# Marks of used channels made on chip, and the down marks scattered with the gate pieces, in a gated attention and feed-forward block

## The chip, the core and the metric

The kernel runs on one core of a Trainium2 chip. Its engines are TensorE (PE, with its weight loads shown as PEld), VectorE (DVE), ScalarE (ACT), GpSimd (POOL) and SyncE (SP, which here only issues DMAs). The metric is the device time of one execution in microseconds (us). For the kernel before, the median of three runs is 751.65 us (749.36 to 752.27).

## What is computed

The reference takes x (8 batches, 256 rows, 512 channels), applies a layer norm and cross-attention with 16 heads to a context of 256 rows, adds the result through a tanh gate, and then a feed-forward part with 1408 inner channels. The feed-forward part quantises to fp8, and it reorders channels by two index lists before it does so:

```python
def _qlinear(qx, scale_x, scale, W, idx, out_idx=None):
    Wr = W[:, idx]
    w_scale = jnp.max(jnp.abs(Wr), axis=1, keepdims=True) / FP8_MAX
    qw = _fp8(Wr / w_scale)
    y = qx * scale_x @ (qw * w_scale).T * scale
    if out_idx is not None:
        y = y[:, out_idx]
    return y
...
qx, sx, sc = _reorder_quantize_x(xf, up_reorder_index)
g = _qlinear(qx, sx, sc, w_gate, up_reorder_index, out_idx=down_reorder_index)
u = _qlinear(qx, sx, sc, w_up, up_reorder_index, out_idx=down_reorder_index)
t = jax.nn.silu(g) * u
qt, st, sct = _reorder_quantize_x(t, down_reorder_index)
y = _qlinear(qt, st, sct, w_down, down_reorder_index)
```

The row maxima are taken over the channels that an index list names. A list may in principle name a channel twice and another never. The kernel therefore needs marks: for each of the 512 input channels whether `up_reorder_index` names it, and for each of the 1408 inner channels whether `down_reorder_index` does. A weight row is multiplied by the marks before its maximum is taken.

## The kernel before

All work is in tiles of 128 partitions. A batch of x is two such tiles of 512 channels. The program has a first part (loads, the four attention weights, keys, values and queries of batch 0), a middle part, and the feed-forward part at the end. The middle part loops over 8 batches with 8 pairs of heads each. For a pair it forms scores on PE (L528), subtracts the row maximum on DVE (`sn`, L543), takes the exponential on ACT (`pr`, L553), transposes (L569) and multiplies by the values (L587). Between the pairs stand slots that hold the projections of the next batch, and "pieces" of the feed-forward weights: 11 rows of tiles of the gate weight (`prep_up`, L344), then a gather of the whole by the up index (`gather_up`, L360), the same for the up weight, then four pieces of the down weight (`prep_down`, L370) and its gather. The source order is only a wish: a scheduler moves instructions between the engines' queues as their dependences allow, and each engine then runs its own queue in order. A DMA is queued on the engine that issues it: SP, ACT or POOL.

What the change and the steps of the prediction touch:

- The small loads on ACT's queue: the biases bq_c, bk_c, bv_b, bo_b (L110 to L116), the two gates (L118, L119), then the index lists `d_i` (L121) and `u_i` (L123), one word per element. ACT takes the tanh of the gates (`tg`, L724), DVE copies it (L725) and scales bo_b with it.
- `dd_i` (L137): eleven gathers on POOL that look the down index up in itself; POOL issues them as soon as d_i has landed. The gate pieces load their rows by dd_i (L346).
- `mark_held` (L321): it fills a small table in DRAM with zeros (L323), then scatters ones into it, 128 at a time (L328), each waiting for the one before since all write the same table. It is called for `held_u` (512 words, 4 scatters) and `held_d` (1408 words, 11 scatters), after the o weight is prepared.
- `load_held` (L337): SP loads held_u, spread over all partitions, as `mu_b` (L338), and held_d as `md_f` (L340), which DVE copies to `md_b` in bf16 (L341).
- A gate or up piece: POOL gathers the rows (L346) and multiplies them by mu_b (L352), DVE takes the maximum (L186), ACT and DVE quantise. The normalised x of each batch is multiplied by mu_b too (L676). A down piece: SP loads `wd` (L372), which shares one buffer with md_f, and DVE multiplies it by md_b (L373).
- The queries: PE multiplies (L485), DVE scales into `qT` (L492), POOL adds the bias (L495). The first scores need this. POOL also adds bo_b to x (L659).

Of the kernel before, what the change touches and what calls it, by code (L numbers as in the profile page):

```python
# [29 lines left out]
F32 = mybir.dt.float32  # L30
BF16 = mybir.dt.bfloat16
FP8 = mybir.dt.float8e4
I32 = mybir.dt.int32
U32 = mybir.dt.uint32
AF = mybir.ActivationFunctionType
ALU = mybir.AluOpType
# [4 lines left out]
P = 128  # L41
# [10 lines left out]
def tile_flamingo_block(  # L52
# [22 lines left out]
    nc = tc.nc  # L75
    B, S, C = x.shape
# [4 lines left out]
    KC = C // P  # L81
    IC = I // P
# [13 lines left out]
    dram = ctx.enter_context(tc.tile_pool(name="dram", bufs=1, space=DRAM))  # L96

    def ctile(shape, name, dt=F32):
        return const.tile(shape, dt, tag=name, name=name)
# [4 lines left out]
    def load_x(b):  # L104
        nc.sync.dma_start(
            x_sb[:, b * TPB : (b + 1) * TPB, :], x[b].rearrange("(t p) c -> p t c", p=P)
        )

    bq_c = ctile([P, KC], "bq_c")
    nc.scalar.dma_start(bq_c, bq.rearrange("(k p) -> p k", p=P))  # L110
    bk_c = ctile([P, KC], "bk_c")
# [5 lines left out]
    gate = ctile([P, 2], "gate")  # L117
    nc.scalar.dma_start(gate[:, 0:1], g_xattn.partition_broadcast(P))  # L118
    nc.scalar.dma_start(gate[:, 1:2], g_ffn.partition_broadcast(P))  # L119
    d_i = ctile([P, IC], "d_i", I32)  # L120
    nc.scalar.dma_start(d_i, down_idx.rearrange("(k p) -> p k", p=P))  # L121
    u_i = ctile([P, KC], "u_i", I32)
    nc.scalar.dma_start(u_i, up_idx.rearrange("(k p) -> p k", p=P))  # L123

    ident = ctile([P, P], "ident")
    make_identity(nc, ident)
# [2 lines left out]
    zeros = ctile([P, IC], "zeros")  # L129
    nc.vector.memset(zeros, 0.0)  # L130
    ones = ctile([P, 1], "ones")
    nc.vector.memset(ones, 1.0)


    dd_i = ctile([P, IC], "dd_i", I32)
    for k in range(IC):
        nc.gpsimd.indirect_dma_start(  # L137
            out=dd_i[:, k : k + 1],
            out_offset=None,
            in_=down_idx.rearrange("(r e) -> r e", e=1),  # L140
            in_offset=bass.IndirectOffsetOnAxis(ap=d_i[:, k : k + 1].bitcast(U32), axis=0),
# [6 lines left out]
    mu_b = ctile([P, C], "mu_b")  # L148
# [5 lines left out]
        n: dram.tile([C, I], BF16, tag=f"scr_{n}", name=f"scr_{n}") for n in ("gate", "up")  # L154
    }
    scr_d = dram.tile([I, C], BF16, tag="scr_d", name="scr_d")
    held_u = dram.tile([C, 1], F32, tag="held_u", name="held_u")
    held_d = dram.tile([I, 1], F32, tag="held_d", name="held_d")
    scr_x = [dram.tile([C, S], BF16, tag=f"scr_x{b}", name=f"scr_x{b}") for b in range(B)]

    def fp8_grid(rp, src, rs, dst, n, name):

        v = rp.tile([P, n], F32, tag="r_v", name=f"v_{name}")
        nc.scalar.activation(v, src, AF.Identity, scale=rs)  # L164
        a = rp.tile([P, n], FP8, tag="r_a", name=f"a_{name}")
        nc.scalar.activation(a, v, AF.Abs, scale=0.5, saturate=False)
        q = rp.tile([P, n], FP8, tag="r_q", name=f"q_{name}")
        nc.vector.tensor_scalar(q, v, F8_MAX, -F8_MAX, ALU.min, ALU.max, saturate=False)  # L168
        nc.vector.scalar_tensor_tensor(dst, a, F8_MAX / 2, q, ALU.max, ALU.mult)  # L169

    def scale_of(pool, mx, s, name):

        nc.vector.tensor_scalar(s, mx, R448, None, ALU.mult)  # L173
        rs = pool.tile([P, s.shape[-1]], F32, tag="rs", name=f"rs_{name}")
        nc.vector.reciprocal(rs, s)  # L175
        return rs
# [8 lines left out]
    def absmax(dst, src):  # L185
        nc.vector.tensor_reduce(dst, src, AX.X, ALU.max, apply_absolute_value=True)  # L186

    with ExitStack() as actx:
# [3 lines left out]
        at = actx.enter_context(tc.tile_pool(name="at", bufs=2))  # L192
        rp = actx.enter_context(tc.tile_pool(name="rp", bufs=2))
        one = actx.enter_context(tc.tile_pool(name="one", bufs=1))
        sm = actx.enter_context(tc.tile_pool(name="sm", bufs=4))
# [3 lines left out]
        def bank(name, dt=F32):  # L199
            n = 512 if dt == F32 else 1024  # L200
            return ps_m.tile([P, n], dt, tag="m", name=name)
# [33 lines left out]
        def norm_steps(t0, t1):  # L235
            steps = [partial(norm_stats, t) for t in range(t0, t1)]
            steps += [partial(norm_rstd, t0, t1)]
            steps += [partial(norm_max, t) for t in range(t0, t1)]
            return steps + [partial(norm_scales, t0, t1)]
# [20 lines left out]
        def prep_fp32(n, rows):  # L260
            for k in range(KC):
                wr = rows[k]
                pt = bank(f"pt_{n}{k}")
                for cc in range(KC):
                    nc.tensor.transpose(
                        pt[:, cc * P : (cc + 1) * P], wr[:, cc * P : (cc + 1) * P], ident
                    )
                nc.scalar.copy(
                    wTf[n][:, :, k * P : (k + 1) * P], pt.rearrange("p (c o) -> p c o", o=P)
                )  # L270
# [6 lines left out]
        def transpose_bf16(src, dst, n, name):  # L277

            pt = bank(f"tb_{name}", BF16)
            for k in range(n):  # L280
                nc.tensor.transpose(
                    pt[:, k * P : (k + 1) * P], src[:, k * P : (k + 1) * P], ident_b
                )
            nc.any.tensor_copy(dst, pt[:, : n * P].rearrange("p (k o) -> p k o", o=P))  # L284
# [10 lines left out]
        def prep_int8(n, tiles):  # L295
            for k, wr in enumerate(tiles):
                sk = s8[n][:, k : k + 1]
                absmax(sk, wr)
                rs = int8_scale(sm, sk, sk, f"w{n}{k}")
                qw = at.tile([P, C], BF16, tag="q8", name=f"qw_{n}{k}")  # L300
                round_int8(wr, rs, qw, f"w{n}{k}")
                transpose_bf16(qw, wT8[n][:, :, k * P : (k + 1) * P], KC, f"w{n}{k}")
# [15 lines left out]
                nc.vector.tensor_copy(dst[:, k0 * P : (k0 + m) * P], pb[:, : m * P])  # L318


        def mark_held(table, idx, n_idx):  # L321

            ins = nc.gpsimd.dma_start(  # L323
                table.rearrange("(k p) e -> p (k e)", p=P), zeros[:, :n_idx]
            )
            tc.keep_in_program_order(ins)
            for k in range(n_idx):
                nc.gpsimd.indirect_dma_start(  # L328
                    out=table[:, :],
                    out_offset=bass.IndirectOffsetOnAxis(  # L330
                        ap=idx[:, k : k + 1].bitcast(U32), axis=0
                    ),
                    in_=ones,
                    in_offset=None,
                )

        def load_held():  # L337
            nc.sync.dma_start(mu_b, held_u.rearrange("c e -> (c e)").partition_broadcast(P))  # L338
            md_f = one.tile([P, I], F32, tag="wd", name="md_f")
            nc.sync.dma_start(md_f, held_d.rearrange("c e -> (c e)").partition_broadcast(P))  # L340
            nc.vector.tensor_copy(md_b, md_f)  # L341


        def prep_up(n, w, k):  # L344
            wr = ld.tile([P, C], F32, tag="wr", name=f"wr_{n}{k}", bufs=2)
            nc.gpsimd.indirect_dma_start(  # L346
                out=wr,
                out_offset=None,
                in_=w,
                in_offset=bass.IndirectOffsetOnAxis(ap=dd_i[:, k : k + 1].bitcast(U32), axis=0),  # L350
            )
            nc.gpsimd.tensor_tensor(wr, wr, mu_b, ALU.mult)  # L352
            mx = sm.tile([P, 1], F32, tag="mx", name=f"mx_{n}{k}")
            absmax(mx, wr)
            rs = scale_of(sm, mx, s_w[n][:, k : k + 1], f"{n}{k}")
            qw = at.tile([P, C], BF16, tag="q8", name=f"q_{n}{k}")
            fp8_grid(rp, wr, rs, qw, C, f"{n}{k}")
            transpose_bf16(qw, wT[n][:, :, k * P : (k + 1) * P], KC, f"{n}{k}")
# [344 lines left out]
            rows_o.append(wr)  # L703
        for b in range(1, B):
            load_x(b)
        prep_fp32("k", rows_k)
        for f in norm_steps(0, TPB):
            f()
# [8 lines left out]
        for f in steps[LC + KC :]:  # L717
            f()
        prep_int8("o", rows_o)
        mark_held(held_u, u_i, KC)  # L720
        mark_held(held_d, d_i, IC)
        load_held()
        tg = wp.tile([P, 2], F32, tag="tg", name="tg")
        nc.scalar.activation(tg, gate, AF.Tanh)  # L724
        nc.vector.tensor_copy(gate, tg)  # L725
# [5 lines left out]

        so_b = wp.tile([P, C], F32, tag="so_b", name="so_b")

        pieces = [partial(prep_up, "gate", w_gate, k) for k in range(IC)]
        pieces += [partial(gather_up, "gate")]
        pieces += [partial(prep_up, "up", w_up, k) for k in range(IC)]
        pieces += [partial(gather_up, "up")]
        pieces += [partial(prep_down, k) for k in range(KC)] + [gather_down]

        def spread(slots, steps, first, end):  # L740
# [35 lines left out]
    with ExitStack() as fctx:  # L776
# [40 lines left out]
        for b in range(B):  # L817
            xg = fx.tile([P, KC, S], BF16, tag="xg", name=f"xg_{b}")
            for k in range(KC):
                nc.gpsimd.indirect_dma_start(  # L820
                    out=xg[:, k, :],
                    out_offset=None,
                    in_=scr_x[b][:, :],
                    in_offset=bass.IndirectOffsetOnAxis(ap=u_i[:, k : k + 1].bitcast(U32), axis=0),
                )
            for nt in range(TPB):
                t = b * TPB + nt
                tt = fw.tile([P, I], F32, tag="tt", name=f"tt_{t}")
                for half in range(2):
                    ph = {}  # L830
                    for n in ("gate", "up"):
                        ph[n] = ps_g.tile([P, 2, 512], F32, tag=n, name=f"p_{n}_{t}_{half}")
                        for j in range(2):
                            c0 = half * HI + j * QI
                            for k in range(KC):
# [4 lines left out]
                                    start=(k == 0),  # L840
                                    stop=(k == KC - 1),
# [15 lines left out]
                    up = fw.tile([P, HI], F32, tag="up", name=f"up_{t}_{half}")  # L857
# [88 lines left out]
```

## Time and profile before

| | us |
|---|---|
| median of three runs | 751.65 |
| profiled execution | 753.15 |
| its span | 751.4 |
| PE busy | 525.7 |
| DVE busy | 548.2 |
| ACT busy | 415.0 |
| POOL busy | 278.9 |

The span is what the profiler saw between the first and the last instruction; the profiled execution is 1.75 us longer than it. Busy times are sums over the span, and do not say which engine another one waits for. That is read from three other views: the busy time of each engine in chosen stretches of the span, the list of who waited for whom, and the timeline, in which a bracket at the end of a line gives the idle time of that engine just before the instruction and what released it. DMA-issuing instructions appear under the queue of their engine (SPq, ACTq), and those of POOL under POOL.

### The profile page before, as it was taken

Reading aid. Unit: us, or ns where it says so; the run is one execution under the profiler, and the core shown is the slowest. Engines: PE = TensorE matmul, PEld = TensorE weight load, DVE = VectorE, ACT = ScalarE, POOL = GpSimd, SP = SyncE. Lnnn points to the kernel's source line nnn. Section 1 sums busy time; section 2 is a strip of 40 time slices with the busy share of each in tenths; the row PEclk is TensorE's granted clock in tenths of the full one; section 3 lists DMA queues with packets and bytes.
Section 4 is the critical chain, followed back from the end, with each engine's and each line's share of the span. In section 5 each row is a group of like instructions: output and inputs, shape, how many; then the busy total and the mean of one; then the engine's idle time right before and its main releaser. Section 6 shows DMA issues by size and latency. Waiting matters only on the chain. (4 is left out here: it accounts for less than half of the span.)

```text
span 751.4 us, 10398 instructions
## 1 busy us (share of the span) xinstructions
PE 525.7 (70%) x3561; PEld 341.6 (45%) x3584; DVE 548.2 (73%) x1429; ACT 415.0 (55%) x957; POOL 278.9 (37%) x241
## 2 busy tenths in 40 slices
PE   3850867878978877788876765743857767777762
PEld 2620645645646545556455534431634434444421
DVE  2951789798797798797869873755567676978970
ACT  3450876858658678578576654552235434545540
POOL 3622355235135152330121015103455566655440
PEclk9995889999999989999898888766789899989985
DMA  8823031112034011010241123000100010000000
GB/s 270 305 14 42 1 120 45 41 28 85 2 117 136 1 57 57 17 55 29 92 130 39 39 78 92 1 15 14 43 14 32 25 42 29 32 25 29 30 14 28
DMA packets 27157, 42.59 MB, mean 57 GB/s; under 512 B 6528, under 2 KB 14080, under 8 KB 27104
## 3 DMA queue, kind: packets, MB, share of 16 engines
q1 hardware_dynamic: 18656, 29.17, 11.6%
q0 software_dynamic: 4864, 12.22, 6.5%
q10 hardware_dynamic: 3584, 0.54, 0.4%
q8 instruction: 28, 0.46, 0.2%
q14 instruction: 25, 0.20, 0.1%
HBM read 31.28 MB, written 10.63 MB: 56 GB/s over the span
## 5 line engine op out<-in xcount | busy, mean ns | idle before, releaser
L553 ACT ACTIVATE pr<-sn,nm 128x256 f32<-128x256 f32 x256 | 128.3, 505 | 58.1 <-DVE nm L543 45.4
L543 DVE CUSTOM_DVE_ANT_0 sn<-s,mk 128x256 f32<-128x256 f32 x256 | 98.4, 416 | 13.8 <-PE s L528 5.5
L569 PE MATMUL t<-ident,pr 128*128 128x128 f32 x512 | 83.6, 314 | 26.6 <-DVE woT L284 23.6
L836 PEld LDWEIGHTS <-xg 128*128 128x128 bf16 x512 | 52.8, 104 | 74.7 <-issue 34.8
L569 PEld LDWEIGHTS t<-ident,pr 128*128 128x128 f32 x512 | 69.4, 164 | 31.6 <-DVE woT L284 23.8
L868 POOL TENSOR_TENSOR tt<-up,sl 128x704 f32<-128x704 f32 x32 | 62.9, 1967 | 39.6 <-DVE up L858 23.8
L836 PE MATMUL p_up<-upT,xg 128*128 128x352 bf16 x256 | 51.8, 340 | 20.8 <-DVE up L858 18.2
L424 PE MATMUL pk<-cT,wkT 128*128 128x256 f32 x256 | 64.1, 403 | 2.4 <-issue 2.4
L495 POOL TENSOR_SCALAR qT<-qT,bq_c 128x256 f32<-128x256 f32 x32 | 17.7, 557 | 128.4 <-DVE qT L492 128.2
L836 PE MATMUL p_gate<-gateT,xg 128*128 128x352 bf16 x256 | 49.2, 337 | 14.7 <-DVE gs L849 7.9
L440 PE MATMUL pv<-wvT,cT 128*128 128x512 f32 x128 | 58.6, 603 | 0.0
L424 PEld LDWEIGHTS pk<-cT,wkT 128*128 128x128 f32 x256 | 50.7, 205 | 9.7 <-issue 2.7
L578 DVE COPY pT<-t 128x512 f32<-128x512 f32 x64 | 44.0, 687 | 11.3 <-PE t L569 7.7
L186 DVE TENSOR_REDUCE mxt<-tt 128x1 f32<-128x1408 f32 x16 | 25.9, 1620 | 33.6 <-POOL tt L868 33.6
L553 ACT ACTIVATION_READ_ACCUMULATOR pr<-sn,nm 128x1 f32 x256 | 49.0, 191 | 0.0
L528 PE MATMUL s<-kT,qT 32*128 32x256 f32 x512 | 41.3, 433 | 9.3 <-DVE nm L543 7.9
L576 ACT COPY pT<-t 128x512 f32<-128x512 f32 x64 | 37.0, 578 | 18.7 <-PE t L569 14.0
L883 ACT COPY qtT<-ptq 128x1024 bf16<-128x1024 bf16 (+1 forms) x32 | 22.3, 748 | 44.0 <-PE ptq L880 42.4
L886 PE MATMUL yp<-wdT,qtT 128*128 128x512 bf16 x161 | 42.6, 413 | 5.1 <-ACT qtT L883 3.1
L164 ACT ACTIVATE v_t<-tt,rs_t 128x1408 f32<-128x1408 f32 x16 | 23.5, 1468 | 39.7 <-DVE sy L890 39.7
L587 PE MATMUL poT<-pT,v 128*32 128x256 f32 x512 | 41.4, 450 | 2.0 <-DVE pT L578 1.0
L893 POOL TENSOR_TENSOR yo<-yo,x_sb 128x512 f32<-128x512 f32 x16 | 21.6, 1347 | 53.7 <-issue 44.3
(187 smaller groups left out, 1166.7 us busy)
## 6 DMA issues: line engine op xcount, KB each, us to landing
cr<-in_ctx_dram SPq DMA_DIRECT2D x8, 512.0 KB
x_sb<-in_x_dram SPq DMA_DIRECT2D x8, 512.0 KB
out_dram<-yo SPq DMA_DIRECT2D x16, 256.0 KB
wd<-in_L_ffn_w_down_dram SPq DMA_DIRECT2D x4, 704.0 KB
mk<-in_mask_BxSxS_ff_dram SPq DMA_DIRECT2D x8, 256.0 KB
scr_x<-x2T SPq DMA_DIRECT2D x8, 256.0 KB
scr_gate<-gateT SPq DMA_DIRECT2D x1, 1408.0 KB
scr_up<-upT SPq DMA_DIRECT2D x1, 1408.0 KB
```

The source lines that it names most:

```text
L424: nc.tensor.matmul(pk[:, :L], wTf["k"][:, cc, oc * P : (oc + 1) * P], cT[:, cc, :], start=(cc == 0), stop=(cc == KC - 1),)
L440: nc.tensor.matmul(pv, cT[:, cc, lt * P : (lt + 1) * P], wTf["v"][:, cc, :], start=(cc == 0), stop=(cc == KC - 1),)
L528: return nc.tensor.matmul(pss[h][:, nt, :], qT[r0 : r0 + D, oc, nt * P : (nt + 1) * P], kT[r0 : r0 + D, oc, :], start=True, stop=True,)
L543: nc.vector.tensor_tensor_reduce(out=sn[:, nt, :], in0=pss[h][:, nt, :], in1=mk[:, nt, :], scale=-1.0, scalar=3.0e38, op0=ALU.add, op1=ALU ...
L553: nc.scalar.activation(pr[:, nt, :], sn[:, nt, :], AF.Exp, bias=nm[:, nt : nt + 1], scale=-1.0, accum_out=sums[:, nt, h : h + 1],)
L569: nc.tensor.transpose(pst[:, lc, nt * P : (nt + 1) * P], pr[:, nt, lc * P : (lc + 1) * P], ident,)
L576: nc.scalar.copy(pT, pst)
L578: nc.vector.tensor_copy(pT, pst)
L587: return nc.tensor.matmul(poT[oc][r0 : r0 + D, :], v[0][:, lc, h * D : (h + 1) * D], probsT[h][:, lc, :], start=(lc == 0), stop=(lc == LC ...
L836: nc.tensor.matmul(ph[n][:, j, :QI], xg[:, k, nt * P : (nt + 1) * P], wT[n][:, k, c0 : c0 + QI], start=(k == 0), stop=(k == KC - 1),)
L868: nc.gpsimd.tensor_tensor(tt[:, cols], up, sl, ALU.mult)
L886: nc.tensor.matmul(py, qT[:, k, :], wdT[:, k, :], start=(k == 0), stop=(k == IC - 1))
```

## The change

The up marks are no longer kept in DRAM. POOL writes the numbers 0 to 511 into every partition (iota). DVE compares them with each column of u_i, which gives ones where a channel is named; PE multiplies by ones and sums over partitions and columns, so that each partition has a count of each channel; DVE limits it to 1, and that is mu_b. This is written ahead of the k weight's preparation. The down marks stay in DRAM, but the fill is written ahead of the list of pieces, each gate piece is written with one scatter, and the load of md_f is a piece of its own after the gather of the up weight. The loads of the two index lists go to the head of ACT's queue.

```diff
+    d_i = ctile([P, IC], "d_i", I32)
+    nc.scalar.dma_start(d_i, down_idx.rearrange("(k p) -> p k", p=P))
+    u_i = ctile([P, KC], "u_i", I32)
+    nc.scalar.dma_start(u_i, up_idx.rearrange("(k p) -> p k", p=P))
     bq_c = ctile([P, KC], "bq_c")
...
-    d_i = ctile([P, IC], "d_i", I32)
-    nc.scalar.dma_start(d_i, down_idx.rearrange("(k p) -> p k", p=P))
-    u_i = ctile([P, KC], "u_i", I32)
-    nc.scalar.dma_start(u_i, up_idx.rearrange("(k p) -> p k", p=P))
...
+    one_b = ctile([P, 1], "one_b", BF16)
+    nc.vector.memset(one_b, 1.0)
...
-    held_u = dram.tile([C, 1], F32, tag="held_u", name="held_u")
...
-        def mark_held(table, idx, n_idx):
-
-            ins = nc.gpsimd.dma_start(
-                table.rearrange("(k p) e -> p (k e)", p=P), zeros[:, :n_idx]
+        def held_up():
+
+            iota = one.tile([P, C], F32, tag="xm", name="iota")
+            nc.gpsimd.iota(
+                iota, [[1, C]], base=0, channel_multiplier=0, allow_small_or_imprecise_dtypes=True
             )
-            tc.keep_in_program_order(ins)
-            for k in range(n_idx):
-                nc.gpsimd.indirect_dma_start(
-                    out=table[:, :],
...
-        def load_held():
-            nc.sync.dma_start(mu_b, held_u.rearrange("c e -> (c e)").partition_broadcast(P))
+            u_f = sm.tile([P, KC], F32, tag="u_f", name="u_f", bufs=1)
+            nc.vector.tensor_copy(u_f, u_i)
+            pc = bank("count_u")
+            for k in range(KC):
+                oh = at.tile([P, C], BF16, tag="q8", name=f"oh_{k}")
+                nc.vector.tensor_scalar(oh, iota, u_f[:, k : k + 1], None, ALU.is_equal)
+                nc.tensor.matmul(
+                    pc, one_b.to_broadcast([P, P]), oh, start=(k == 0), stop=(k == KC - 1)
+                )
+            nc.vector.tensor_scalar(mu_b, pc, 1.0, None, ALU.min)
+
+        def mark_down(k):
+
+            nc.gpsimd.indirect_dma_start(
+                out=held_d[:, :],
+                out_offset=bass.IndirectOffsetOnAxis(ap=d_i[:, k : k + 1].bitcast(U32), axis=0),
+                in_=ones,
+                in_offset=None,
+            )
+
+        def load_down_marks():
             md_f = one.tile([P, I], F32, tag="wd", name="md_f")
             nc.sync.dma_start(md_f, held_d.rearrange("c e -> (c e)").partition_broadcast(P))
             nc.vector.tensor_copy(md_b, md_f)
...
+        held_up()
         prep_fp32("k", rows_k)
...
         prep_int8("o", rows_o)
-        mark_held(held_u, u_i, KC)
-        mark_held(held_d, d_i, IC)
-        load_held()
...
-        pieces = [partial(prep_up, "gate", w_gate, k) for k in range(IC)]
+        nc.gpsimd.dma_start(held_d.rearrange("(k p) e -> p (k e)", p=P), zeros)
+
+        def gate_piece(k):
+            mark_down(k)
+            prep_up("gate", w_gate, k)
+
+        pieces = [partial(gate_piece, k) for k in range(IC)]
         pieces += [partial(gather_up, "gate")]
         pieces += [partial(prep_up, "up", w_up, k) for k in range(IC)]
-        pieces += [partial(gather_up, "up")]
+        pieces += [partial(gather_up, "up"), load_down_marks]
         pieces += [partial(prep_down, k) for k in range(KC)] + [gather_down]
```

More of the change, by code (lines that the diff above doesn't have):

```diff
@@ L318, in row_bcast @@
                 nc.vector.tensor_copy(dst[:, k0 * P : (k0 + m) * P], pb[:, : m * P])
-        def mark_held(table, idx, n_idx):
-            ins = nc.gpsimd.dma_start(
-                table.rearrange("(k p) e -> p (k e)", p=P), zeros[:, :n_idx]
-            )
-            tc.keep_in_program_order(ins)
-            for k in range(n_idx):
-                nc.gpsimd.indirect_dma_start(
-                    out=table[:, :],
[L330 to L334, printed above, removed]
-                )
-        def load_held():
-            nc.sync.dma_start(mu_b, held_u.rearrange("c e -> (c e)").partition_broadcast(P))
+        def held_up():
+            iota = one.tile([P, C], F32, tag="xm", name="iota")
+            nc.gpsimd.iota(
+                iota, [[1, C]], base=0, channel_multiplier=0, allow_small_or_imprecise_dtypes=True
+            )
+            u_f = sm.tile([P, KC], F32, tag="u_f", name="u_f", bufs=1)
[6 more added lines that the diff above has]
+                    pc, one_b.to_broadcast([P, P]), oh, start=(k == 0), stop=(k == KC - 1)
+                )
+            nc.vector.tensor_scalar(mu_b, pc, 1.0, None, ALU.min)
[7 more added lines that the diff above has]
+        def load_down_marks():
             md_f = one.tile([P, I], F32, tag="wd", name="md_f")
```

## The prediction

> **What bounds the kernel now.** I read three views of the profile: the busy time by stage, the waits of one stretch, and the timeline of that stretch. The page's chain of waits covers only its last few per cent, so it doesn't help here. The slices on the page show one hole, in the fourth of 40 slices; the stages around it are these (columns: stretch, its length, busy us of PE, PE weight load, DVE, ACT, POOL, then the granted TensorE clock, DMA share, GB/s).
>
> ```profile
> 22.00:36.00 14.00, 11.27 (x86) 9.45 (x89) 12.71 (x40) 6.93 (x13) 8.75 (x12) 0.99 0.95 333
> 36.00:46.00 10.00, 9.12 (x52) 4.70 (x53) 10.00 (x38) 5.82 (x18) 1.50 (x2) 1.00 0.41 21
> ...
> 52.00:57.00 5.00, 0.00 (x0) 0.00 (x0) 0.00 (x0) 0.72 (x1) 2.84 (x3) 0.61 0.01 0
> 57.00:69.00 12.00, 0.00 (x0) 0.00 (x0) 0.00 (x0) 0.00 (x0) 0.23 (x1) 0.50 0.27 9
> 69.00:72.00 3.00, 0.00 (x0) 0.00 (x0) 0.00 (x0) 0.00 (x0) 1.73 (x2) 0.50 0.83 221
> ...
> 75.00:97.00 22.00, 18.91 (x112) 13.78 (x114) 17.69 (x55) 18.45 (x50) 9.03 (x10) 0.88 0.01 1
> ```
>
> From 52 to 72 us no compute engine does anything; before and after it, PE and DVE are each 80 to 100% busy, from 75 us ACT too. So the kernel is bound by these engines together, with a hole of 20 us in it. The waits say on what:
>
> ```profile
> DVE mx_gate L186 <- POOL wr_gate L352: 24.3, 1, 24.3
> PEld t L569 <- DVE woT L284: 23.8, 1, 23.8
> ...
> ACT pr L553 <- DVE nm L543: 21.0, 1, 21.0
> POOL held_d L328 <- DMA held_d<-zeros: 12.9, 1, 12.9
> POOL held_u L328 <- DMA held_u<-ones,u_i: 5.9, 3, 2.5
> ```
>
> DVE waits for the first product of a gate piece with mu_b on POOL, PE and ACT wait for DVE, and POOL waits for its own small writes to DRAM. The timeline has the order:
>
> ```profile
> 35.66 0.83 POOL L323 DMA_DIRECT2D held_u<-zeros  x1
> ...
> 46.29 1.00 POOL L328 DMA_INDIRECT held_u<-ones,u_i  x1 [8.49 <-DMA held_u<-zeros]
> 49.75 1.00 POOL L328 DMA_INDIRECT held_u<-ones,u_i  x1 [2.46 <-DMA held_u<-ones,u_i]
> ...
> 56.10 1.13 POOL L323 DMA_DIRECT2D held_d<-zeros  x1
> 57.48 0.34 SPq L338 DMA_DIRECT2D mu_b<-held_u  x1
> 57.93 0.37 SPq L400 DMA_DIRECT2D cr<-in_ctx_dram  x1
> 70.10 1.02 POOL L328 DMA_INDIRECT held_d<-ones,d_i  x1 [12.87 <-DMA held_d<-zeros]
> 71.29 1.26 POOL L352 TENSOR_TENSOR wr_gate<-wr_gate,mu_b 128x512 f32<-128x512 f32 x1 [0.17 <-DMA mu_b<-held_u]
> 72.59 0.69 DVE L186 TENSOR_REDUCE mx_gate<-wr_gate 128x1 f32<-128x512 f32 x1 [24.30 <-POOL wr_gate L352]
> ```
>
> The reader should see that one fill of held_d (1408 single words) takes 12.9 us to land, that a scatter costs its own 1.0 us and some 1.4 more before the next may start, and that mu_b and cr, issued right behind the fill, moved only once it was through (9 GB/s until 69, then 221).
>
> **What the Trainium skill says.** "DMA: Bandwidth & Descriptors", section Specifications, has transfers under 512 B as read-modify-writes; its section Queues, rings and completion order says that an engine goes round its queues by whole packets, of up to 64 descriptors. Both agree with the 9 GB/s and the stalled mu_b and cr above. "Trainium Kernel Development and Optimization", section Key Constraints, says that transfers of all issuing queues share the same 16 engines: so the fill, wherever it is put, competes with the loads of that time. "Perfetto Trace Analysis", section Per-engine timelines, calls DVE, ACT and GpSimd strict first in, first out; the hole above is just that.
>
> **The change, part by part.** Its sum is made against the profiled execution (753.15 us, span 751.4), 1.5 above the median of 751.65; a difference in us carries over to the median.
>
> 1. Removed: the fill of held_u (0.83 on POOL, landed 9.8 later), its four scatters (46.3 to 56.1) and the load of mu_b. With mu_b made on chip early, POOL's first product no longer waits, and the hole as it is now goes, up to 21 us.
>
> 2. Added for the marks: an iota on POOL (the affine select of a quarter of the size took 0.29, so some 1.2, in POOL's idle time before 12 us); four comparisons of 128x512 on DVE (like the 0.48 of L274), a copy, and a minimum (the 0.69 of L318): about 3 us; four matmuls of 128x512 (0.41 each at L886): 1.7 us. d_i and u_i now lead ACT's queue. bq_c, 512 words, landed at about 5.1 (ACT's sixth issue, at 5.09, waits for it) and bk_c 1.0 later (SP's wait for it ends at 6.1), so 32 words on each engine take 1.0: d_i with 88 lands at 6.9 by this, at 7.4 by the 6.2 that it took before; I take 7.1, against 12.15. The tanh gate comes some 4 later (13 against 9.05), and DVE and ACT queue behind it, and SP's next loads slip by about 2. All this costs 3 to 4 us if nothing covers it. Item 3 covers it.
>
> 3. Moved: the held_d scatters. They are written beside the gate pieces, but the instruction order of the built program has them otherwise. On POOL it is, in short:
>
> ```
> dd_i gathers x11, fill of held_d, scatters 1-6 (two x_sb adds between),
> gathers of wr_gate0 and 1, qT x3, scatter 7, qT, products with mu_b x2, scatters 8-11
> ```
>
> Before, the qT steps (33.86) stood ahead of every fill. qT feeds the first scores, on which PE, then DVE and ACT stand in order. And SP's md_f waits for scatter 11, its copy to md_b stands on DVE ahead of the scores of the second group (sn, L543), which ran at 73.34 before. So one hole becomes two, on one chain:
> - d_i at 7.1; eleven gathers took 13.9 (12.15 to 26.06): 21.0; the fill's issue, 0.3 + 1.13: 22.4.
> - The fill lands after Z.
> - Scatters 1 to 6: three steps of 2.4 and two of 2.7 (2.9 and 2.5 with a product between, before), so 12.6 to the start of the sixth; its own 1.0 and two gathers of 1.3: 16.2 until qT.
> - qT x3 1.4, scatter 7 1.1, qT 0.5, two products 2.6, then 8 to 11 at 2.4: the last starts 13.2 after qT. md_f is issued 2.3 later (96.09 to 98.37), lands 4.1 after that, the copy takes 1.0: 20.6.
> - c: scatters 2 to 6 fall in the time of the bulk loads. Held_u's first intervals were 3.5 and 2.9 beside one gather; c is 0 to 3, I take 1.5.
>
> DVE resumes at 22.4 + Z + 16.2 + 20.6 + c = 59.2 + Z + c. DVE's own work from qT to there is about 15 (33.9 to 48.3 before), less than 20.6, so POOL stays the bound. By then DVE has done three reductions of 0.68, some small steps and the copy (3.5 together) that came later before, ACT two passes of 0.72 (1.4): credit 2.3. The load of wd_0 (about 4.2) is issued there; 4.5 us of DVE work lie before its use. So
>
> difference = 59.2 + Z + c - 73.3 - 2.3 = Z + c - 16.4.
>
> Z is what the trace doesn't show, a fill of 1408 words beside bulk loads. From below: 512 words took 9.8, so not under that. From above: that fill shared the engines and cost 19 ns a word against 9.1 for held_d, and at that price 1408 words take 27. I take 12.9, since mu_b and cr stood in line behind the fill of before without moving. Difference: 12.9 + 1.5 - 16.4 = -2.0. The bulk loads (333 GB/s from 22 to 36) then stall until 35 and end near 47; the wo and x rows that DVE needs ahead of qT arrive by 38 and qT on DVE by 43, still ahead of POOL's 52.
>
> 4. The rest: held_d's chain on POOL until 97 goes, but nothing waited for it then (the next POOL step waited for ACT, 1.64). There is one piece more to spread, and a few POOL steps change places in the later batches: zero, within 2 either way.
>
> **Rivals.**
> - Forecast: the hole moves ahead of qT and md_b, nearly as long: 749.7. For it: the order, and 12.9. Its own range is 745 to 755.
> - B, the chain is shorter: Z as for 512 words, 9.8, c 0, credit 3.5: -7.8, or 743.9. For it: 27% DMA share during the fill, so little real work; against: 12.9 was measured.
> - C, slower: each word of the fill alternates with the bulk loads on the same engines. It is between the bounds at Z 20 and c 3: +6.6, 758.3; at 27, 765. It decides from Z + c = 16.4, and is past 0.5% from 20.2. For it: held_u's price per word; against: mu_b and cr stood still.
> - That the change doesn't do what it says is partly in the forecast: the scatters don't lie along the gate pieces. Were md_b not in DVE's way, 20.6 would be 15: -7.6, near B; the order speaks against it.
>
> **How the numbers follow.** 0.5% is 3.8 us, about what a measurement tells from no change. Forecast 0.42 (0.18 faster, 0.21 within, 0.03 slower), B with its like 0.30 (faster), C 0.28 (slower). Faster 0.48, same 0.21, slower 0.31. The range goes to B with 5 more for the later batches and md_b, 739, and into C up to Z 24 with c 3 (+10.6), 762.
>
> **What would show it.** Right: no idle stretch after mu_b, a POOL wait on held_d's fill from 22 us of about 13, PE idle until qT at 52 to 55, DVE idle before md_b until 73 to 76, and GB/s near zero during the fill. Wrong: a fill that lands before 32 or after 42, scores that start before 45, or a DVE that passes md_b without waiting. If the first 110 us come out as said and the time doesn't, the later batches did it.

## The result, and the profile after

Over 16 runs each, the changed kernel took 753.19 us (median, 750.29 to 754.58) against 749.59 of the kernel before (747.02 to 753.11). The ratio is 1.0031, 95% interval 1.0015 to 1.0048: slower by about 2.3 us by this ratio (the two medians differ by 3.6). The repeat in the first experiment gave 1.0017 (1.0002 to 1.0031), about 1.3 us. So the change costs 1.3 to 2.3 us, and the forecast had it at 2.0 faster.

The profiled execution of the changed kernel took 751.51 us (span 749.7). It lies at the low end of that kernel's runs, and the profile of the kernel before (753.15) at the high end of its own: the two profiles, compared whole, point the wrong way. They are therefore compared stage by stage, and against second profiles.

The opening first. Busy time by stretch, profile after (columns as in the prediction):

```profile
26.00:32.00 6.00, 4.70 (x13) 3.81 (x14) 6.00 (x23) 2.13 (x5) 0.00 (x0) 0.55 1.05 74
32.00:42.00 10.00, 8.54 (x65) 7.12 (x64) 7.93 (x27) 5.38 (x10) 2.25 (x3) 1.00 0.93 294
42.00:54.00 12.00, 1.94 (x18) 1.70 (x16) 5.92 (x17) 3.34 (x5) 7.67 (x8) 0.77 0.02 3
...
57.00:69.00 12.00, 10.95 (x60) 5.83 (x56) 10.29 (x41) 8.19 (x23) 7.04 (x8) 0.93 0.01 1
69.00:75.00 6.00, 2.97 (x16) 2.27 (x16) 0.37 (x1) 3.27 (x5) 0.00 (x0) 1.00 0.37 122
```

The 57 to 69 stretch, in which nothing ran before, is now full. In its place PE has 1.9 us of work in the twelve from 42 to 54, and DVE 0.4 in the six from 69 to 75. From 26 to 32 the DMA engines are busy (mean share 1.05) and move 74 GB/s; in the same six microseconds of the kernel before they moved 372:

```profile
26.00:32.00 6.00, 3.49 (x33) 2.54 (x32) 4.75 (x15) 3.98 (x8) 2.56 (x3) 1.00 1.06 372
```

From 32 to 42 the stopped loads catch up (294). The waits of the first 110 us, after:

```profile
POOL held_d L341 <- DVE mv L214: 13.1, 1, 13.1
POOL held_d L341 <- DMA held_d<-ones,d_i: 13.0, 6, 5.0
...
PE s L538 <- POOL qT L505: 11.1, 1, 11.1
```

The first of these is the first scatter behind the fill. The view names DVE's `mv` as its releaser, but `mv` isn't an input of the scatter: a wait put down to whatever ended about then. What the scatter needs is the fill that was issued just ahead of it; that this is the wait is inferred here, and experiment 2 changes the fill to test it. The next ones wait another 13.0 us for each other, and PE waits 11.1 for qT, which stands on POOL behind six of them. The timeline of the same kernel shows the chain:

```profile
20.46 1.14 POOL L742 DMA_DIRECT2D held_d<-zeros  x1
...
34.71 1.01 POOL L341 DMA_INDIRECT held_d<-ones,d_i  x1 [13.11 <-DVE mv L214]
40.74 0.97 POOL L341 DMA_INDIRECT held_d<-ones,d_i  x1 [5.02 <-DMA held_d<-ones,d_i]
...
50.94 0.96 POOL L341 DMA_INDIRECT held_d<-ones,d_i  x1 [1.43 <-DMA held_d<-ones,d_i]
54.51 1.39 POOL L505 TENSOR_SCALAR qT<-qT,bq_c 128x256 f32<-128x256 f32 x3
...
70.11 0.34 SPq L350 DMA_DIRECT2D md_f<-held_d  x1
74.63 0.89 DVE L351 CAST md_b<-md_f 128x1408 bf16<-128x1408 f32 x1 [5.77 <-DMA md_f<-held_d]
75.44 0.42 DVE L553 CUSTOM_DVE_ANT_0 sn<-s,mk 128x256 f32<-128x256 f32 x1
```

The scores of the second group start at 75.44, against 73.34 before: in this pair of profiles the two holes cost 2.1 us more than the one. By the time the fourth batch begins (its first row subtraction `sn`, the 97th of 256) the changed kernel is at 218.63 against 221.05, so 2.4 ahead. So far the forecast holds. At the seventh batch it stands at 379.63 against 374.62: 5.0 behind. This pair puts what went wrong between the fourth and the seventh batch, not in the opening; one pair alone doesn't show it.

### The profile page after: what moved, and what is told of

It reads as the page before. It is cut to its first block, busy times and chain, and to the rows that moved or that the text cites. A ratio compares the mean times of both kernels' runs of the same rounds, so it can differ in the third digit from the quotient of the medians.

```text
span 749.7 us, 10414 instructions
## 1 busy us (share of the span) xinstructions
PE 529.4 (71%) x3565; PEld 341.6 (46%) x3588; DVE 550.4 (73%) x1437; ACT 415.6 (55%) x956; POOL 272.2 (36%) x237
## 5 line engine op out<-in xcount | busy, mean ns | idle before, releaser
L850 PE MATMUL p_up<-upT,xg 128*128 128x352 bf16 x256 | 51.9, 340 | 20.9 <-DVE up L872 18.3
L450 PE MATMUL pv<-wvT,cT 128*128 128x512 f32 x128 | 61.5, 627 | 0.0
L434 PEld LDWEIGHTS pk<-cT,wkT 128*128 128x128 f32 x256 | 50.4, 204 | 12.9 <-ACT cT L427 5.6
L538 PE MATMUL s<-kT,qT 32*128 32x256 f32 x512 | 42.0, 439 | 18.6 <-POOL qT L505 11.1
L669 POOL TENSOR_TENSOR x_sb<-x_sb,bo_b 128x512 f32<-128x512 f32 x16 | 21.3, 1336 | 58.2 <-ACT xq L474 58.0
```

Of the source, the lines that this page charges most:

```text
L434: nc.tensor.matmul(pk[:, :L], wTf["k"][:, cc, oc * P : (oc + 1) * P], cT[:, cc, :], start=(cc == 0), stop=(cc == KC - 1),)
L450: nc.tensor.matmul(pv, cT[:, cc, lt * P : (lt + 1) * P], wTf["v"][:, cc, :], start=(cc == 0), stop=(cc == KC - 1),)
L538: return nc.tensor.matmul(pss[h][:, nt, :], qT[r0 : r0 + D, oc, nt * P : (nt + 1) * P], kT[r0 : r0 + D, oc, :], start=True, stop=True,)
L850: nc.tensor.matmul(ph[n][:, j, :QI], xg[:, k, nt * P : (nt + 1) * P], wT[n][:, k, c0 : c0 + QI], start=(k == 0), stop=(k == KC - 1),)
```

## The experiments

Each kernel was timed in turn with the kernel before on the same chip; ratios are to that. Theory P, mine: the opening is worth the forecast 2 us, and the thirtieth piece, which changes how the pieces fall to batches, takes more than that back. The rivals stand in the texts on record.

**1. Where the loss is: second profiles, and the number of pieces swapped.** Two kernels were run again unchanged, and two with one edit each.

> The changed kernel as it is, to have it beside the others on one chip and to have a second profile of it. Both theories: 1.003 of the kernel before (about 752 us to 749.6). Theory P (the thirtieth piece): the landmarks of the first 110 us come again within 1 us (qT at 54.5, the scores of the second group at 75.4, those of the fifth at 122.8), and the places between 270 and 380 us lag the kernel before by 2 to 5 us again. Theory O (the opening differs from run to run, and the first profile showed a good one): the fill takes 2 to 5 us longer to land than 13.1, or the scatters under load take longer than the 16.2 us that the first six took, and the scores of the second group start past 78.

> The kernel before as it is, for a second profile, since its first one lay 1.5 to 3.5 us above its median. Theory P and theory O both: 747 to 753 us, the scores of the second group at 73.3 within 1. If the later batches of one kernel differ by 3 us or more between its own two profiles, the lag of 2 to 5 us between 270 and 380 us can't be read from one pair of profiles, and the timed pairs with 29 and 30 pieces decide.

The kernel before with one empty piece more:

```diff
-        pieces += [partial(gather_up, "up")]
+        pieces += [partial(gather_up, "up"), lambda: None]
```

> The kernel before with an empty thirtieth piece behind the gather of the up weight, so that its pieces are spread over the batches as in the changed kernel; nothing else differs. Theory P: slower than before by 2 to 5 us, ratio 1.003 to 1.006, with the first 110 us as before. Theory O: 1.000 within 0.001.

The changed kernel with one piece fewer:

```diff
-        pieces += [partial(gather_up, "up"), load_down_marks]
+        def gather_up_and_marks():
+            gather_up("up")
+            load_down_marks()
+
+        pieces += [gather_up_and_marks]
```

> The changed kernel with the load of the down marks joined to the gather of the up weight in one piece, so that there are 29 as before; the opening is the same instruction for instruction on GpSimd up to the marks. Theory P: the 2 us that the opening gains are seen, ratio 0.996 to 0.999 of before, 3 to 5 us below the changed kernel. Theory O: as the changed kernel, 1.002 to 1.004.

Measured: the changed kernel 753.68 us, 1.0017 (1.0002 to 1.0031); the kernel before with 30 pieces 758.04, **1.0068** (1.0043 to 1.0092); the changed kernel with 29 pieces 750.44, **0.9966** (0.9947 to 0.9984); the kernel before 752.78. An empty piece costs 5.3 us in the one kernel (2 to 5 were expected), and the thirtieth piece 3.2 in the other (753.68 less 750.44). Without it the change gains 2.3, and 2.0 was forecast. Theory O expected the second group past 78; it starts at 75.44, 75.13 and 76.10 in the three profiles that share this opening. The two of the changed kernel were quick executions (751.51 is low among its 16 runs, 750.0 the lowest of 22), so it is the timed pairs, in which only the number of pieces differs, that decide against O.

The second profile of the kernel before missed its expectation: its second group starts at 77.68, not within 1 of 73.3, and its seventh batch at 378.25, where the second profile of the changed kernel has 378.18. The lag of 5.0 at that place is not in this pair.

What the thirtieth piece changes is a whole-number division. A batch b takes the pieces from `len(pieces) * b // 7` on: with 29 of them from 0, 4, 8, 12, 16, 20, 24; with 30 from 0, 4, 8, 12, 17, 21, 25. The fourth batch gets a fifth up row. Lengths of the batches, each from its first `sn` to the next batch's, read from the timelines of the six profiles (us):

| | before | before again | before, 30 | after | after again | after, 29 |
|---|---|---|---|---|---|---|
| fourth | 51.7 | 51.4 | 55.5 | 56.6 | 56.6 | 50.1 |
| fifth | 51.6 | 51.7 | 52.5 | 51.6 | 51.6 | 51.3 |
| sixth | 50.3 | 50.3 | 53.0 | 52.8 | 52.8 | 51.0 |
| seventh | 69.7 | 66.6 | 65.1 | 63.2 | 63.1 | 68.6 |
| sum | 223.3 | 220.0 | 226.2 | 224.2 | 224.2 | 220.8 |

With 30 pieces the fourth batch is 4 to 6.5 us longer and the sixth 2 to 3; the seventh gives back 1.5 to 5.5, and the sums differ by 3.3 (after) and 4.5 (before, mean of two profiles), near the 3.2 and 5.3 of the times. The seventh is the uncertain one: it alone makes the sums of the two profiles of the kernel before differ by 3.3. The fourth to sixth together are not: 152.3 to 153.6 us in the three profiles with 29 pieces, 161.0 to 161.1 in the three with 30. And from the start of the eighth batch to the end all six take the same, 306.8 to 307.1 us. The same batches by engine, first the fourth batch with 30 pieces (kernel before), then with 29 (kernel before):

```profile
225.68:281.21 55.53, 41.30 (x324) 27.85 (x324) 45.33 (x136) 35.80 (x101) 20.35 (x20) 0.97 0.22 65
```

```profile
221.05:272.77 51.72, 41.23 (x316) 28.96 (x316) 41.96 (x138) 34.68 (x99) 18.10 (x18) 0.90 0.22 65
```

DVE has 3.4 us more to do there: of the products of up rows with mu_b, four fall into the batch instead of three. The work is moved, not added. Over the four batches of the table DVE is busy for 187.5 to 187.7 us with 30 pieces and 186.9 to 187.6 with 29, so the longer sum is waiting. The wait that is new in this batch, from the view of the waits of the 30-piece kernel:

```profile
DVE mx_up L186 <- POOL wr_up L352: 4.1, 1, 4.1
```

DVE stands 4.1 us at the maximum of an up row whose product POOL hasn't made yet; with 29 pieces no such wait is among the batch's longer ones. The seventh batch has the same five down pieces either way, but with 30 the gather of the up weight, which with 29 ran at 377 to 382 in the seventh batch of the kernel before, runs at 366 to 371 in the sixth. POOL's work in the seventh falls from 11.65 to 7.13 (first 29 pieces, then 30, kernel before):

```profile
374.62:444.30 69.68, 49.30 (x349) 33.71 (x348) 58.22 (x165) 47.94 (x121) 11.65 (x12) 0.84 0.18 56
```

```profile
386.74:451.83 65.09, 45.48 (x317) 31.62 (x322) 56.48 (x157) 45.59 (x118) 7.13 (x7) 0.80 0.12 38
```

That the thirtieth piece costs the 3 to 5 us is shown by the timed pairs. Why the seventh batch gives back less than the fourth and sixth take is not shown.

**2. What the opening's hole is made of.** Four kernels. In the first, the fill, each scatter, and the load and copy of the down marks are held at their place in the source:

```diff
+        fill = nc.gpsimd.dma_start(held_d.rearrange("(k p) e -> p (k e)", p=P), zeros)
+        tc.keep_in_program_order(fill)
...
+            ins = nc.gpsimd.indirect_dma_start(
...
+            tc.keep_in_program_order(ins)
...
+            ins = nc.sync.dma_start(
+                md_f, held_d.rearrange("c e -> (c e)").partition_broadcast(P)
+            )
+            tc.keep_in_program_order(ins)
+            tc.keep_in_program_order(nc.vector.tensor_copy(md_b, md_f))
```

> The changed kernel with the fill, each scatter and the load and copy of the down marks kept at the place where the source writes them, so that neither qT nor the scores stand behind them; 30 pieces as in the changed kernel. Theory P (the change is good, its order and its thirtieth piece spoil it): qT within 3 us of 33.9 and the scores of the second group at 53 to 58 instead of 75.4, no idle stretch of over 4 us between 40 and 75; 16 to 20 us below the changed kernel, ratio to before 0.974 to 0.982. Theory Q (the hole is due to data, such as a late transfer that the fill slows, and follows the fill): a hole of about 13 us behind the fill stays, wherever GpSimd has it, and the gain over the changed kernel is below 8.

The second holds only the load and the copy (the last five lines of that diff):

> The changed kernel with only the load of the down marks and their copy kept at their place in the source; fill and scatters still ahead of qT. Theory P: the first hole stays (qT at 54.5), the second goes: DVE, which has about 15 us of its own work between qT and the scores of the second group, reaches these at about 70 instead of 75.4; 4 to 6 us below the changed kernel, ratio 0.994 to 0.999. Theory Q or any in which the second half of the hole is POOL's gate products and not the marks' copy: no change, 1.002 to 1.004.

The third and fourth change the layout of the fill, of held_d in the changed kernel and of both tables in the kernel before. The zeros are the same, only which partition writes which words differs:

```diff
-        nc.gpsimd.dma_start(held_d.rearrange("(k p) e -> p (k e)", p=P), zeros)
+        nc.gpsimd.dma_start(held_d.rearrange("(p k) e -> p (k e)", p=P), zeros)
```

> The changed kernel with the fill of the down marks written as 128 rows of eleven neighbouring words instead of 1408 single words, at the same place on GpSimd's queue. Theory P (the fill's landing is the price of its words, and the chain through qT and the marks is on the path): the first scatter waits 2 to 4 us instead of 13.1, qT and the scores of the second group come 8 to 11 us earlier, 7 to 10 us below the changed kernel, ratio 0.990 to 0.995; the bulk loads no longer stop between 26 and 34 us. Theory Q' (the fill waits in line behind the bulk loads, whatever its form): it lands after 9 to 13 us all the same, ratio 1.002 to 1.004.

> The kernel before with both fills written as rows of neighbouring words (128 rows of 4 and of 11). Theory P: both landings drop from 9.8 and 12.9 to 2 to 4, the product with the up marks comes 14 to 18 us earlier, and DVE's wait of 24.3 for it falls below 10; 13 to 18 us below before, ratio 0.976 to 0.983, with the time of the stretch from 57 to 72 gone. Theory Q' (a small fill takes its 10 to 13 us whatever its form): 1.000.

Measured, with the kernel before at 751.54: everything held 747.46, 0.9945 (0.9923 to 0.9966); load alone held 757.67, 1.0097 (1.0059 to 1.0136); rows in the changed kernel 745.47, 0.9927 (0.9895 to 0.9958); rows in the kernel before 735.40, **0.9801** (0.9764 to 0.9838).

The times of the two kernels with rows came out as theory P has them. In the kernel before the scatter now starts 2.3 us after the start of the fill's issue, and DVE's wait for the product with mu_b is 7.4 instead of 24.3 (timeline of the kernel before with rows):

```profile
49.62 0.59 POOL L323 DMA_DIRECT2D held_d<-zeros  x1
50.84 0.34 SPq L338 DMA_DIRECT2D mu_b<-held_u  x1
51.91 1.00 POOL L328 DMA_INDIRECT held_d<-ones,d_i  x1 [1.70 <-DMA held_d<-zeros]
55.69 1.26 POOL L352 TENSOR_TENSOR wr_gate<-wr_gate,mu_b 128x512 f32<-128x512 f32 x1 [2.78 <-DMA mu_b<-held_u]
56.99 0.69 DVE L186 TENSOR_REDUCE mx_gate<-wr_gate 128x1 f32<-128x512 f32 x1 [7.38 <-POOL wr_gate L352]
```

The layout alone, without the change, is worth about 15 us (0.9801 of 751.5; 12 to 18 by the interval). The Trainium skill has a reason in "DMA: Bandwidth & Descriptors", section Rules for kernel authors: a last dimension that isn't contiguous becomes one descriptor per element. Here 1408 single words took 12.9 us, and the same bytes as 128 rows took 1.7 from the end of their issue. The profiles count packets, not descriptors (27157 in all before, 27141 with rows), so the number of descriptors itself is not shown. In the changed kernel with rows the bulk loads went on (374 to 386 GB/s from 22 to 34 us), but the scatters now ran beside them (timeline of that kernel):

```profile
20.12 0.60 POOL L742 DMA_DIRECT2D held_d<-zeros  x1
...
26.31 0.99 POOL L341 DMA_INDIRECT held_d<-ones,d_i  x1 [5.58 <-DVE sx L187]
32.14 0.96 POOL L341 DMA_INDIRECT held_d<-ones,d_i  x1 [4.85 <-DMA x_sb<-in_x_dram]
36.75 1.22 POOL L341 DMA_INDIRECT held_d<-ones,d_i  x1 [2.35 <-DMA held_d<-ones,d_i]
```

The first scatter waited 5.6 us, not the 2 to 4 expected. It came 8.4 us earlier, but the next two steps took 5.8 and 4.6 instead of 2.4, so the second group of scores (68.62) gained only 6.8 of the 8 to 11 expected.

Both held kernels missed their numbers. Their openings went the way of theory P: held wholly, the second group starts at 58.22 with no hole behind the fill (theory Q falls, though the gain over the changed kernel is as small as Q had it), and with the load alone held at 70.54, 4.9 earlier than in the changed kernel. But qT, which was to come within 3 us of 33.9, comes at 42.8 when all is held; experiment 3 takes that up.

With the load alone held, the 4.9 us have shrunk to 0.4 by the second batch (122.40 against 122.84). The second hole wasn't idle for every engine: the changed kernel enters its second group with 2.3 us more of PE's work done and 3.5 more of ACT's. Later the seventh batch takes 67.9 us against 63.2, and the copy of the marks shows what moved (timeline of the kernel with the load held):

```profile
377.23 0.88 DVE L354 CAST md_b<-md_f 128x1408 bf16<-128x1408 f32 x1
378.14 0.35 SPq L385 DMA_DIRECT2D wd<-in_L_ffn_w_down_dram  x1
382.50 1.63 DVE L386 TENSOR_TENSOR wd<-wd,md_b 128x1408 f32<-128x1408 f32 x1 [1.63 <-DMA wd<-in_L_ffn_w_down_dram]
385.73 1.61 DVE L187 TENSOR_REDUCE mx_d<-wd 128x1 f32<-128x1408 f32 x1
```

The one buffer that md_f shares with `wd` comes free only after the copy. So the first down row is loaded at 378.1, and its maximum is at 385.7 instead of 375.0. My expectation had left out that the early copy, which makes the second hole, also frees the buffer early. That this is the 4.7 us of the seventh batch is argued from the order; experiment 3 tests it on the wholly held kernel.

**3. The parts put right one after another.** Each kernel adds one edit to the one above it; the first is the wholly held kernel with the load and copy free again.

> As the kernel with everything pinned, but the load and copy of the down marks left to the scheduler (it puts the copy between the fill's eleven scatters and the first down row, about half way through DVE's middle part); 30 pieces. Theory L (the late load costs: with it the first down row was loaded only at 370.8, and DVE and PE waited through the sixth and seventh batch): 5 to 7 us below the pinned kernel, ratio 0.984 to 0.990, and the stretch between the scores of the seventh and the eighth batch (sn192 to sn224) back from 68.9 to about 63. Theory M (the pinned kernel's lost gain is all the thirtieth piece and clock): no change, 0.993 to 0.996.

> The same with the load of the down marks joined to the gather of the up weight, so 29 pieces. Theory P: a further 3 to 5 us, ratio 0.977 to 0.984, about what the opening gains (16 us at the scores of the third group) less nothing. Theory M', in which the thirtieth piece only matters for the order that the changed kernel has: no further gain.

The third moves two things back or later:

```diff
-    d_i = ctile([P, IC], "d_i", I32)
-    nc.scalar.dma_start(d_i, down_idx.rearrange("(k p) -> p k", p=P))
-    u_i = ctile([P, KC], "u_i", I32)
-    nc.scalar.dma_start(u_i, up_idx.rearrange("(k p) -> p k", p=P))
     bq_c = ctile([P, KC], "bq_c")
...
     nc.scalar.dma_start(gate[:, 1:2], g_ffn.partition_broadcast(P))
+    d_i = ctile([P, IC], "d_i", I32)
+    nc.scalar.dma_start(d_i, down_idx.rearrange("(k p) -> p k", p=P))
+    u_i = ctile([P, KC], "u_i", I32)
+    nc.scalar.dma_start(u_i, up_idx.rearrange("(k p) -> p k", p=P))
...
-        held_up()
         prep_fp32("k", rows_k)
...
         prep_int8("o", rows_o)
+        held_up()
```

> The same with the index loads back behind the biases and the gates, and the comparisons and products for the up marks written after the preparation of the o weight instead of ahead of the k weight. Theory S (these two moves hold up the start by 9 us, which the hole covers in the changed kernel: qT at 42.8 in the pinned one against 33.9 before): qT at 34 to 36, a further 6 to 9 us, ratio 0.967 to 0.974. Rival: the fill, now issued at about 27 among the bulk loads and ahead of the weights that qT needs, stops these for its 13 us, qT at 40 or later, and the ratio stays at 0.977 or above.

> The same with the fill written as 128 rows of eleven neighbouring words. If the single-word fill stops the bulk loads in the kernel before this one and its wait is on the path, this one is faster by 3 to 8 us, ratio 0.962 to 0.968, and the throughput from 26 to 40 us doesn't drop below 150 GB/s; if the fill is hidden there, the two are equal within 2 us.

| | us | ratio | interval | second group starts |
|---|---|---|---|---|
| all held (experiment 2) | 747.46 | 0.9945 | 0.9923 to 0.9966 | 58.22 |
| load free | 742.97 | 0.9899 | 0.9848 to 0.9949 | 56.74 |
| and 29 pieces | 736.98 | 0.9799 | 0.9747 to 0.9851 | 57.38 |
| and the start as before | 731.39 | **0.9729** | 0.9678 to 0.9779 | 52.91 |
| and the fill in rows | 733.60 | 0.9769 | 0.9720 to 0.9819 | 50.11 |

The kernel before was at 751.54 for the first row and at 749.78 for the others. The free load gives 0.0046, about 3.4 us, where theory L had 5 to 7; the two were timed on different chips and their intervals overlap, so this gain is not clear of the noise, though the seventh batch took 65.2 against 68.9 (about 63 was expected). The 29 pieces give 6.0 us, a little more than the 3 to 5 expected, and the start gives 5.6, below the 6 to 9 expected. The intervals of neighbouring rows overlap for these two as well, since each holds the scatter of the kernel before; the runs themselves don't (742.8 to 745.0, 734.5 to 739.3, 729.5 to 732.1). qT comes at 37.17 and not at 34 to 36: the fill is issued at 26.25 among the bulk loads, and from 30 to 38 the DMA engines are busy (mean share 1.19) while their rate falls to 222 and then 97 GB/s. Rows bring qT to 34.38, but that profile had moved more (299 against 260 GB/s) already by 22 us, ahead of either fill, so the difference isn't the fill's alone. In the time rows don't show: the two are equal within their intervals.

The version with the start as before (731.39) beats the kernel before by 18.4 us and the changed one by more; the kernel before with its fills in rows (0.9801, in the series of experiment 2) comes within a per cent of it by a change of layout alone.

## Why the prediction was wrong

By its own steps:

- **Item 1, the old hole goes**: as said. DVE's wait for the product with mu_b is gone.
- **Item 2, the start**: put at 3 to 4 us if nothing covers it. It is covered in the changed kernel, as item 3 says. Uncovered, in experiment 3, moving both back gained 5.6 us, with the fill moved forward by the same step; so it was mis-sized, with no effect on the forecast. The iota took 0.55 us and not 1.2.
- **Item 3, the new chain**: the mechanism was right, in order and place. Its terms: the fill's issue ended at 21.6 (22.4 forecast); Z 13.1 (12.9); c 3.6 (1.5, bounds 0 to 3); from qT to the second group 20.9 (20.6). DVE resumed at 75.4 (73.6). c was the mis-sized term (3.6 to 4.3 in the four profiles of this opening): one step of 6.0 us, while the bulk loads that the fill had stopped caught up. One sum was slightly off too: the terms given for the last scatter add up to 12.8, not 13.2. The credit, the work already done by then, was 4.5 and not 2.3 (bounds 1.4 to 3.5): from the second group to the fourth batch the kernel before took 147.71 us and the changed one 143.19, and DVE's busy time in it fell by 4.26 (124.75 to 120.49). The other profiles put that stretch at 147.2 and 150.4 with the old opening and 142.0 and 144.3 with the new. So two terms were outside their bounds with opposite signs, and it is luck that the opening was worth 2.3 us in timed runs of the 29-piece kernel (1.2 to 4.0 by the interval), against 2.0. The 73.3 that the sum starts from was itself one profile's: 75.2 and 77.7 stand in two others with the old opening, a spread wider than the forecast difference.
- **Item 4, "one piece more to spread [...] zero, within 2 either way"**: this is the step that failed. The thirtieth piece cost 3.2 us in the changed kernel, and 5.3 alone in the kernel before. The zero had no reason beside it. The diff and the loop that spreads the pieces were enough to see that the fourth batch gets a fifth row. The profile of before would not have given the size: DVE is 81% busy in that batch (41.96 of 51.72) and 84% in the seventh (58.22 of 69.68), and it is the fourth that grew. I priced the operations that change and not where the others fall.
- **Rivals**: B (Z 9.8) and C (Z 20 or more) are both refuted by 13.1. C's mechanism was there in reverse: the fill kept its 13 us, and the bulk loads waited for it. The last rival held in its description, since scatters and md_b did stand ahead of qT and `sn`; taking md_b out of the way brought the second group to 70.5, 4.9 earlier, close to the 5.6 implied (20.6 less 15). But all but 0.4 of it was gone by the second batch, and the kernel ended slower than the changed one.
- The last sentence of the prediction's test was the right one: the first 110 us came out as said in order, the time did not, and the later batches did it. On the size: forecast 2.0 faster, measured 2.3 slower; of that gap of 4.3 the thirtieth piece is 3.2, and the rest is within the intervals.

## What to carry to other kernels

When a change alters the length of a list that is divided over stages, write out the old and the new division, and time the kernel before with an empty step added: that prices the new division alone, which the busy shares here did not. A step that is written beside other work only lies there if the instruction order of each queue says so; an in-order queue turns a scheduler's early placement into a hole. And before moving a small slow transfer about, look at its layout: here the same bytes in rows were worth more than the whole change.

## What was not expected of the hardware

The single-word fill takes about the same whatever runs beside it: 12.9 and 14.8 us in the two profiles of the kernel before, with nearly nothing beside it, and 13.0 to 14.1 in four profiles amid the bulk loads. There it is the loads that give way (74 GB/s against 372). A scatter of 128 words does slow down: its step is 2.4 us alone and up to 6.3 beside bulk loads. The layout also cuts the time that POOL spends on the fill's issue, from 1.14 to 0.60 us.

The profiles of one kernel differ by up to 4 us in the opening (the second group of the kernel before at 73.34 and 77.68), so a difference of 2 us can't be read from one pair of profiles.
